# Cross-attention with image prompts on one core: the second batch's context turned on VectorE, prompts projected in four column tiles, its inner products ahead of the first products, and the last keys in two column tiles

## The chip, the cores and the metric

The kernel runs on one core of one Trainium2 chip. The metric is device time in microseconds (us) from the first to the last instruction of one execution, taken as the median of several executions. Three executions of the kernel before gave 419.8, 421.6 and 420.98 us: a median of 420.98 us.

## The reference: what is computed

Eight batches of 112 queries with 320 channels attend to 371 text rows and 4 prompt rows of a 512-channel context, in 20 heads of 16 channels. Beside the usual attention there is a second, small one over the 4 prompts. Its scores get an extra term: the cosine between the probability-weighted mean of the text rows (`qsem`) and each prompt.

```python
q, k_t, v_t = heads(x @ W_q), heads(text @ W_k), heads(text @ W_v)
probs_t  = softmax(q @ k_t.T * scale)            # 112 x 371 per head
text_out = probs_t @ v_t
qsem     = l2norm(probs_t @ text)                # 112 x 512 per head
fused    = q @ k_ip.T * scale + 0.5 * qsem @ l2norm(ip).T
probs_ip = softmax(fused) * spatial_mask         # 112 x 4 per head
out = (text_out + probs_ip @ v_ip) @ W_out + b_out + x
```

All data are float32. Every matmul of the program appears in the trace as two MATMUL records, each with its own weight load (a transpose through TensorE as one).

## The kernel before, in words

**Tiling.** `qsem` is never formed. Its length is p G p^T, with p a row of probabilities and G the 371 x 371 matrix of inner products of the context rows ("gram"). So each head needs one product of its turned probabilities with a tile `u` that holds, side by side, G, the products with the normalised prompts, a column of ones and the values. The 20 heads go in five groups of four (steps (b, g), g = 0 to 4). The four heads of a group sit in the four 32-row strips of the array and run beside each other.

**One step (b, g).** `scores` (L662) makes four score tiles from `kT` and the masked queries `qm`. `probabilities` takes the maximum on VectorE (L675) and the exponential on ScalarE (L679), and sends p to a tile `xg` by DMA on the SP queue (L686). `transposed` turns it on VectorE (`xgT`, L698). `product` (L710) is the large product in twelve blocks of 32 context rows. `reduced` multiplies the result by p and sums it on VectorE (L763); `value_sums` copies the small columns on ScalarE (L737). `placed` puts the values of the next step into `u` on GpSimd (L629). Scores run two steps ahead of products.

**Preparing a batch.** `load_ctx` loads the context. For batches 0 and 1 (`b < LEAD`) rows lie on partitions and `transposed_context` turns them by 12 transposes through TensorE with copies from PSUM on ScalarE and VectorE (L414, L422, L424). From batch 2 on it is loaded in 32 x 128 pieces and turned by three VectorE instructions (L402); then `prompts_behind` copies the four normalised prompt columns into the same tile on GpSimd (L390). `gram` (L474) makes G in three pieces, four column tiles of 32 wide beside each other, doubled on ScalarE (L460) and multiplied by `half` on GpSimd (L461), and `gram_to_groups` spreads it over strips of `u` by DMA (L488). `values` (L543) projects V in three chunks; `values_to_dram` and `values_to_groups` reorder it through DRAM. `keys` (L512) projects K in three blocks of 128 channels.

**The last 64 channels.** 320 channels are two full blocks and 64 channels more (heads 16 to 19). The kernel before spreads those four heads over four 32-row strips with zeros between (`spread`, L124). For batches 0 and 7 the third key block is a full 128-wide projection of spread weights (L512, and `last_keys`, L526). For batches 1 to 6 the 64 channels ride along with the values, which are 384 wide for that (L543), go to a spread tile `k3` on GpSimd (L552) and are turned by three TensorE transposes (L503).

**The prompts.** `prompt_projections` projects all 32 prompt rows with two weights, each into its own 32-wide column tile of one bank, 320 columns each (L280); the result goes to `kip` and to DRAM.

**What sets the order.** The order on every engine around the change is written out by hand (`manual_schedule`): an engine takes its instructions in program order and waits at each for the semaphores that it needs. The prologue does batch 0 and step (0, 0); `alone(0)` does the products of step (0, 0); `behind(n)` then does work for the next batch between the products of one step and of the next ones; `pair(n)` does the products of two steps. `turn` names the PSUM pools of the banks that come next. The SP queue has eight completion semaphores in rotation, so that a DMA is issued only when the one eight places ahead of it has landed.

**Lines of the prologue** that the prediction follows. SP loads context 0, the value weights, x of batch 0, the query and key weights and context 1 (L161 to L170). TensorE: gram of batch 0 (L444), values (L543), queries (L344) and keys (L512) of batch 0, scores (0, 0), context 1 (L414), scores (0, 1), two more key blocks, the first piece of gram 1; then the products of (0, 0), two more pieces of gram 1, the prompt projections (L280), a chunk of values 1 and the products of (0, 1). GpSimd clears 64 rows of `xT` (L327), which the third matmul of the first query block needs, and prepares weights.

## Time and profile before

| | |
|---|---|
| executions | 419.8, 421.6, 420.98 us; median 420.98 us |
| the profiled execution's own time | 421.54 us |
| its span, first to last instruction | 419.8 us (1.7 us lie around it) |
| mean granted TensorE clock | 0.999 |
| DMA | 64.64 MB in 58002 packets, 154 GB/s over the span |
| chain that ended last, by engine | PE 87%, DVE 4%, DMA 3%, ACT 2%, SPq 2% |

How to read it: PE is TensorE's matmuls, PEld its weight loads, DVE VectorE, ACT ScalarE, POOL GpSimd, SP SyncE, which issues DMAs here; SPq, ACTq and POOLq are the sequencers' own records, DMA issues above all. A row of the timeline gives start and length in us, engine, line, operation, output<-input, shape and count, and in brackets the idle time of that engine before it and what ended it. A row of the groups gives count, busy us, mean ns of one, idle time. Matmul records overlap, since they are pipelined, so the pace of a group is its busy time over its count, or the difference between the starts of two rows, and not the mean length of one record.

### The profile page before, as it was taken

To read this page: it belongs to the slowest core of one execution; us is meant where nothing else is said; L and a number is where in the kernel's file an instruction comes from. 1 tells how busy PE (TensorE), PEld (TensorE's weight loads), DVE (VectorE), ACT (ScalarE), POOL (GpSimd) and SP (SyncE) were. 2 spreads that over 40 slices of the span, in tenths; PEclk is the share of its full clock that TensorE was granted. 3 is DMA by queue.
4 is the path that set the end of the run, shared out by engine and by line. 5 is a ranking of instruction groups with operands and counts; after the bars stand their busy time and mean duration, and the time that the engine had idled before them with its cause. 6 is when DMAs were issued, how large, how long until landed. Compare 5 with 4: busy or idle time off the path is not lost.

```text
span 419.8 us, 13826 instructions
## 1 busy us (share of the span) xinstructions
PE 411.7 (98%) x5511; PEld 314.1 (75%) x5511; DVE 322.2 (77%) x684; ACT 185.5 (44%) x634; POOL 116.0 (28%) x278
## 2 busy tenths in 40 slices
PE   8999999999999999999999999999999999999995
PEld 8866686877677786868686877778776888776893
DVE  4054777897887876886888897887788897789964
ACT  3253333334543642514553464333643464246772
POOL 4302310031161352012051225102124126005570
PEclk9999999999999999999999999999999999999999
DMA  8678966778554656577645575575656345575311
GB/s 249 163 190 246 220 157 165 180 187 181 133 156 125 169 127 170 143 162 160 174 116 138 148 173 144 156 186 138 164 150 168 92 118 149 156 177 169 98 34 29
DMA packets 58002, 64.64 MB, mean 154 GB/s; under 512 B 19016, under 2 KB 51760, under 8 KB 57938
## 3 DMA queue, kind: packets, MB, share of 16 engines
q1 hardware_dynamic: 57054, 62.32, 58.5%
q8 instruction: 44, 0.72, 0.7%
q10 hardware_dynamic: 692, 0.89, 0.7%
q0 software_dynamic: 192, 0.55, 0.6%
q14 instruction: 20, 0.16, 0.1%
HBM read 19.04 MB, written 5.22 MB: 58 GB/s over the span
## 4 chain that ended last, share of the span: by engine, by line
PE 87%; DVE 4%; DMA 3%; ACT 2%; SPq 2%; issue 1%; ACTq 0%; POOL 0%; DVEq 0%; POOLq 0%
PE ps_qd L710 39%; PE ps_v L543 15%; PE ps_k L512 10%; PE ps_g L474 8%; PE ps_s L662 5%; PE ps_q L344 3%; PE ps_o L867 2%; DMA xg<-p 1%; DVE xgT L698 1%; PE ps_g L444 1%; DMA vr<-vd 1%; ACT p L679 1%; PE ps_c L414 1%; DVE nmx L675 1%; SPq L488 1%; DMA ct<-in_ctx_dram 1%
## 5 line engine op out<-in xcount | busy, mean ns | idle before, releaser
L710 PE MATMUL ps_qd<-u,xgT 32*112 32x40 f32 (+11 forms) x3840 | 215.7, 351 | 0.4 <-DVE xgT L698 0.4
L710 PEld LDWEIGHTS ps_qd<-u,xgT 32*112 32x112 f32 x3840 | 177.4, 172 | 38.4 <-issue 7.1
L698 DVE STREAM_TRANSPOSE xgT<-xg 128x768 f32<-128x768 f32 (+1 forms) x63 | 123.1, 1976 | 7.1 <-DMA xg<-p 7.1
L679 ACT ACTIVATE p<-ps_s,nmx 112x371 f32<-112x371 f32 x160 | 85.6, 584 | 58.3 <-DVE nmx L675 57.2
L675 DVE TENSOR_REDUCE nmx<-ps_s 112x1 f32<-112x371 f32 x160 | 77.1, 534 | 36.7 <-PE ps_s L662 34.0
L763 DVE CUSTOM_DVE_ANT_0 p<-ps_qd,p 112x371 f32<-112x371 f32 x150 | 72.7, 544 | 15.9 <-ACT pvs L737 10.4
L629 POOL COPY u<-vr 128x64 f32<-128x64 f32 x120 | 26.7, 236 | 185.0 <-PE ps_qd L710 108.0
L543 PE MATMUL ps_v<-wv_sb,ctxT 128*128 128x384 f32 (+1 forms) x192 | 63.8, 479 | 0.3 <-ACT kT L519 0.3
L662 PE MATMUL ps_s<-kT,qm 32*112 32x375 f32 (+1 forms) x320 | 60.8, 486 | 0.0
L543 PEld LDWEIGHTS ps_v<-wv_sb,ctxT 128*128 128x128 f32 x192 | 35.3, 190 | 21.2 <-ACT kT L519 1.2
L512 PE MATMUL ps_k<-ctxT,wk_sb 128*128 128x371 f32 x136 | 45.8, 481 | 0.0
L737 ACT COPY pvs<-ps_qd 112x21 f32<-112x21 f32 x150 | 21.7, 198 | 52.4 <-DVE ss L763 50.1
L512 PEld LDWEIGHTS ps_k<-ctxT,wk_sb 128*128 128x128 f32 x136 | 24.6, 190 | 13.4 <-ACT ctxT L424 0.5
L474 PE MATMUL ps_g<-ctxT 128*32 128x119 f32 (+11 forms) x672 | 33.3, 344 | 0.6 <-POOL ctxT L390 0.6
L474 PEld LDWEIGHTS ps_g<-ctxT 128*32 128x32 f32 x672 | 25.9, 109 | 8.1 <-issue 4.1
L662 PEld LDWEIGHTS ps_s<-kT,qm 32*112 32x112 f32 x320 | 27.1, 171 | 5.0 <-issue 0.5
L550 ACT COPY vext<-ps_v 128x384 f32<-128x384 f32 (+1 forms) x24 | 11.2, 465 | 37.1 <-PE ps_v L543 37.0
L681 ACT COPY ipl<-ps_s 112x4 f32<-112x4 f32 x140 | 24.0, 172 | 0.0
L353 DVE TENSOR_SCALAR qm<-ps_q,emask 128x224 f32<-128x224 f32 (+1 forms) x25 | 9.0, 398 | 18.5 <-PE ps_q L344 18.5
L460 ACT ACTIVATE ug<-ps_g 128x375 f32<-128x375 f32 (+2 forms) x24 | 9.0, 377 | 29.2 <-DMA ct<-in_ctx_dram 8.4
L519 ACT COPY kT<-ps_k 128x371 f32<-128x371 f32 x17 | 8.0, 469 | 30.5 <-PE ps_k L512 30.5
L402 DVE STREAM_TRANSPOSE ctxT<-ct 128x512 f32<-128x512 f32 x18 | 19.3, 1077 | 0.0
(157 smaller groups left out, 311.6 us busy)
## 6 DMA issues: line engine op xcount, KB each, us to landing
xg<-p SPq DMA_DIRECT2D x158, 162.3 KB
u<-ug SPq DMA_DIRECT2D x128, 99.0 KB
ct<-in_ctx_dram SPq DMA_DIRECT2D x24, 176.0 KB
vip<-vipd SPq DMA_DIRECT2D x7, 560.0 KB
vr<-vd SPq DMA_DIRECT2D x20, 120.0 KB
vd<-vext SPq DMA_DIRECT2D x14, 160.0 KB
vd<-vext SPq DMA_DIRECT2D x28, 40.0 KB
ct<-in_ctx_dram SPq DMA_DIRECT2D x4, 256.0 KB
```

The source lines that it names most:

```text
L474: nc.tensor.matmul(ps[p * RG : (p + 1) * RG, s0 : T - t0], ctxT[:, e, t0 + q * RG : t0 + (q + 1) * RG], ctxT[:, e, t0 + s0 : T], start=(e ...
L512: nc.tensor.matmul(ps[:, :TT], wk_sb[:, e, i * P : (i + 1) * P], s["ctxT"][:, e, :TT], start=(e == 0), stop=(e == NE - 1),)
L543: nc.tensor.matmul(ps[:, :w], ctxT[:, e, c * P : (c + 1) * P], wv_sb[:, e, :w], start=(e == 0), stop=(e == NE - 1),)
L629: nc.gpsimd.tensor_copy(region(b, c)[:, :, UV - c * P :], s["vr"][:, c * QN : (c + 1) * QN, g, :])
L662: nc.tensor.matmul(ps[:S, :w], qm[a * RG : (a + 1) * RG, i, r, j * S : (j + 1) * S], s["kT"][a * RG : (a + 1) * RG, i, :w], start=True, st ...
L675: nc.vector.tensor_reduce(nmx, ps[:S, :TT], AX.X, ALU.max, negate=True)
L679: nc.scalar.activation(p, ps[:S, :TT], AF.Exp, bias=nmx)
L681: nc.scalar.copy(s["ipl"][:, groups[g][a], :], ps[:S, TT:T])
L698: nc.vector.transpose(xT[:, j : j + n].rearrange("p j (k q) -> p q j k", q=QN), xg[:, :, j * RG : (j + n) * RG].rearrange("p q (j k) -> p ...
L710: nc.tensor.matmul(banks[a][:S, j * RG : UW], xT[a * RG : (a + 1) * RG, j, :S], region(b, c)[a * RG : (a + 1) * RG, p, q * RG :], start=(j ...
L737: nc.scalar.copy(s["pvs"][:, h, :], ps[:S, TT:UW])
L763: nc.vector.tensor_tensor_reduce(out=p, in0=ps[:S, :TT], in1=p, scale=1.0, scalar=0.0, op0=ALU.mult, op1=ALU.add, accum_out=s["ss"][:, h : ...
```

## The change

1. **Context 1** is loaded in pieces (eight DMAs on SP, runs of 512 bytes) and turned by three VectorE instructions, which stand right behind the first gram and ahead of everything else that VectorE does for batch 0. The 12 TensorE transposes and their three copies go. The copy of the prompts (`prompts_behind`) now stands on GpSimd ahead of the clearing of `xT`.
2. **Last keys.** For every batch the third key block is made by `last_keys`: the 64 channels against the two halves of the context rows, in two column tiles of 64 (8 matmuls of 186 or 185 columns), then four copies on ScalarE, each half to two places. The spread weights, `k3`, its transposes and the 64 further columns of the values go; `qm` gets a second mask for that block (one VectorE instruction more for each pair of batches).
3. **Prompt projections** in four column tiles of 160 columns (16 matmuls instead of 8 of 320), with three ScalarE copies and two DMAs to DRAM instead of one each.
4. **Gram of batch 1**: all three pieces ahead of the products of step (0, 0), instead of one ahead and two behind.
5. **Loads**: the prompt weights and x of batches 1 to 4 are issued by GpSimd during the first gram, instead of by SP after the first scores; x of batches 5 to 7 by GpSimd two batches later than before. The weight tiles are now 320 wide, so that a row of the key weights lands in one run.
6. **Sqrt table**: loaded by an instruction of its own right behind the last keys, ahead of where it was loaded.

```diff
     groups = [[i * HC + 2 * a + r for a in range(GROUP)] for i in range(2) for r in range(2)]
-    groups.append([2 * HC + a for a in range(GROUP)])
+    groups.append([2 * HC + 2 * (a % 2) + a // 2 for a in range(GROUP)])
...
-    wk_sb = const.tile([P, NE, CP], F32, tag="wk_sb", name="wk_sb")
-    wv_sb = const.tile([P, NE, C + REST], F32, tag="wv_sb", name="wv_sb")
+    wk_sb = const.tile([P, NE, C], F32, tag="wk_sb", name="wk_sb")
+    wv_sb = const.tile([P, NE, C], F32, tag="wv_sb", name="wv_sb")
...
     def load_ctx(b):
         ct = io.tile([P, NT, E], F32, tag="ct", name=f"ct_{b}")
-        if b >= LEAD:
+        if b > 0:
...
     def prompt_projections():
         ps = bank("ps_kv")
         for e in range(NE):
             for i, w in enumerate((wkip_sb, wvip_sb)):
-                nc.tensor.matmul(
-                    ps[i * N : (i + 1) * N, :C], ipT[:, e, :], w[:, e, :],
-                    start=(e == 0), stop=(e == NE - 1),
-                )
-        kv = work.tile([2 * N, C], F32, tag="vip", name="kv", bufs=1)
-        nc.scalar.copy(kv, ps[: 2 * N, :C])
+                for n, part in enumerate(parts):
+                    m = 2 * i + n
+                    nc.tensor.matmul(
+                        ps[m * N : (m + 1) * N, : C // 2], ipT[:, e, :], w[:, e, part],
+                        start=(e == 0), stop=(e == NE - 1),
+                    )
+        kv = work.tile([P, CP], F32, tag="vip", name="kv", bufs=1)
+        nc.scalar.copy(kv[:N, parts[0]], ps[:N, : C // 2])
+        nc.scalar.copy(kv[:N, parts[1]], ps[N : 2 * N, : C // 2])
+        nc.scalar.copy(kv[2 * N :, : C // 2], ps[2 * N :, : C // 2])
...
-            for r in range(2 if i < FULL else 1):
+            for r in range(2):
                 nc.vector.tensor_scalar_mul(
                     qm[:, i, r, : n * S], ps[:, : n * S], emask[:, r : r + 1]
                 )
...
     def first_gram():
...
             if c == NT - 1:
                 nc.gpsimd.tensor_copy(ctxT[:, :, TT:T], ipnT[:, :, :NIP])
+                load_embed(nc.gpsimd, wkip_sb, w_k_ip)
+                load_embed(nc.gpsimd, wvip_sb, w_v_ip)
+                nc.gpsimd.dma_start(x_sb[:, 1:5, :], x[1:5].rearrange("b s c -> s b c"))
...
     def last_keys(b, ps):
         s = st[b]
         for e in range(NE):
-            nc.tensor.matmul(
-                ps[:, :TT], wk_sb[:, e, FULL * P :], s["ctxT"][:, e, :TT],
-                start=(e == 0), stop=(e == NE - 1),
-            )
-        nc.scalar.copy(s["kT"][:, FULL, :TT], ps[:, :TT])
+            for n in range(2):
+                nc.tensor.matmul(
+                    ps[n * REST : (n + 1) * REST, : min((n + 1) * KH, TT) - n * KH],
+                    wk_sb[:, e, FULL * P :],
+                    s["ctxT"][:, e, n * KH : min((n + 1) * KH, TT)],
+                    start=(e == 0), stop=(e == NE - 1),
+                )
+        for n in range(2):
+            t = slice(n * KH, min((n + 1) * KH, TT))
+            for m in range(2):
+                nc.scalar.copy(
+                    s["kT"][m * REST : (m + 1) * REST, FULL, t],
+                    ps[n * REST : (n + 1) * REST, : t.stop - t.start],
+                )
...
     order_values()
     drain(products)
+    drain(transposed_context(1))
     gram_to_groups(0, range(QN - 1))
...
-    spread(nc.gpsimd, wq_sb)
-    nc.gpsimd.tensor_copy(wv_sb[:, :, C:], wk_sb[:, :, FULL * P : C])
-    spread(nc.gpsimd, wk_sb)
+    nc.gpsimd.tensor_copy(wq_sb[:, :, C:], wq_sb[:, :, FULL * P : C])
...
-    turn[:] = ["mm", "qd", "qd"]
-    drain(transposed_context(1))
-    prompts_behind(1)
     for a in range(GROUP):
         scores(0, 1, a, early=True)
         probabilities(0, 1, a)
-    load_embed(nc.sync, wkip_sb, w_k_ip)
-    load_embed(nc.sync, wvip_sb, w_v_ip)
...
     more_constants()
-    run(("g", 1), lambda: gram(1))
+    turn[:] = ["mm", "mm", "sc"]
+    run(("g", 1), lambda: gram(1), NT)
...
             if n == 0:
-                turn[:] = ["sc", "mm", "qd", "mm"]
-                nc.sync.dma_start(x_sb[:, 1:5, :], x[1:5].rearrange("b s c -> s b c"))
+                turn[:] = ["qd", "mm"]
             else:
                 turn[:] = ["qd"] * 4 + ["mm"]
                 k(b)
+                nc.scalar.preload_act_table(AF.Sqrt)
                 f(b - 1)
...
             tr(0)
-            gr(nb, 2)
             if n:
+                gr(nb, 2)
                 f(b - 1)
```

Here KH is 186, REST is 64 and `parts` are the two halves of the 320 channels. `keys`, which the diff leaves out here, now makes two full blocks and then calls `last_keys` for the third, for every batch but the last one, which calls it at the place where it did before.

More of the change, by code (lines that the diff above doesn't have):

```diff
@@ L241, in order_values @@
             )
-        nc.vector.tensor_copy(
-            wv_by[:, :, :, 2 * FULL, :],
-            wv_in[:, :, FULL * P :].rearrange("p e (a d) -> p e a d", d=D),
-        )
+        last = wv_in[:, :, FULL * P :].rearrange("p e (u v d) -> p e u v d", v=2, d=D)
+        for v in range(2):
+            nc.vector.tensor_copy(wv_by[:, :, 2 * v : 2 * v + 2, 2 * FULL, :], last[:, :, :, v, :])
+    parts = [slice(n * C // 2, (n + 1) * C // 2) for n in range(2)]
     def normalised_prompts():
@@ L310, in prompt_projections @@
         yield
-        nc.sync.dma_start(vipd, kv[N:])
+        for n, part in enumerate(parts):
+            m = 2 + n
+            nc.sync.dma_start(vipd[:, part], kv[m * N : (m + 1) * N, : C // 2])
         yield
@@ L956, in ending @@
             )
-        parts = [slice(i * C // 2, (i + 1) * C // 2) for i in range(2)]
         ps_o = [bank(f"ps_o_{b}_0", spare=True)]
```

81 lines of the change are left out of this document (26 added, 55 removed).

## The prediction

> **What bounds the kernel now.** I read the page first, then who waited for whom on TensorE, then its timeline over the first 50 us.
>
> ```profile
> PE 411.7 (98%) x5511; PEld 314.1 (75%) x5511; DVE 322.2 (77%) x684; ACT 185.5 (44%) x634; POOL 116.0 (28%) x278
> ```
> ```profile
> PE ps_g L474 <- POOL ctxT L390: 0.6, 1, 0.6
> PE ps_qd L710 <- DVE xgT L698: 0.4, 1, 0.4
> ```
>
> TensorE is busy for 411.7 of 419.8 us, and behind its start its longest wait is 0.6 us. So a matmul taken away is worth its length, unless the work behind it then waits for something that it covered. Where that is so is read from the start:
>
> ```profile
> 20.30 0.82 PE L344 MATMUL ps_q<-xT,wq_sb 128*128 128x112 f32 x6
> ...
> 25.91 1.59 PE L414 MATMUL ps_c<-ident,ct 128*128 128x128 f32 x12
> 27.43 1.28 PE L662 MATMUL ps_s<-kT,qm 32*112 32x371 f32 x8
> 28.64 5.25 PE L512 MATMUL ps_k<-ctxT,wk_sb 128*128 128x371 f32 x16
> 33.82 2.71 PE L474 MATMUL ps_g<-ctxT 128*32 128x375 f32 x32
> 36.46 1.22 PE L710 MATMUL ps_qd<-u,xgT 32*112 32x392 f32 x10
> ...
> 41.81 2.31 PE L474 MATMUL ps_g<-ctxT 128*32 128x247 f32 x64
> 43.91 2.36 PE L280 MATMUL ps_kv<-wip,ipT 128*32 128x320 f32 x16
> 46.21 2.85 PE L543 MATMUL ps_v<-wv_sb,ctxT 128*128 128x384 f32 x8
> 48.98 1.22 PE L710 MATMUL ps_qd<-u,xgT 32*112 32x392 f32 x10
> ```
> ```profile
> 25.82 1.95 ACT L679 ACTIVATE p<-ps_s,nmx 112x371 f32<-112x371 f32 x4 [0.52 <-DVE nmx L675]
> ```
> ```profile
> 32.74 3.12 DVE L698 STREAM_TRANSPOSE xgT<-xg 128x768 f32<-128x768 f32 x2 [2.51 <-DMA xg<-p]
> ...
> 42.11 0.54 DVE L763 CUSTOM_DVE_ANT_0 p<-ps_qd,p 112x371 f32<-112x371 f32 x1 [2.11 <-ACT pvs L737]
> ...
> 43.97 4.50 DVE L698 STREAM_TRANSPOSE xgT<-xg 128x1536 f32<-128x1536 f32 x2
> ```
>
> The products of step (0, 0) start at 36.46; their turned probabilities were ready at 32.74 + 3.12 = 35.86. Those of step (0, 1) start at 48.98, behind 7.2 us of other matmuls. VectorE needs nearly as long there: the reductions start at 42.11, the turn at 43.97.
>
> **The price of a column tile of 64.** No row shows one.
>
> ```profile
> L543 PE MATMUL ps_v<-wv_sb,ctxT 128*128 128x384 f32 x144 | 49.8, 492 | 0.0
> ...
> L543 PE MATMUL ps_v<-wv_sb,ctxT 128*128 128x320 f32 x48 | 14.0, 438 | 0.3 <-ACT kT L519 0.3
> ...
> L344 PE MATMUL ps_q<-xT,wq_sb 128*128 128x224 f32 x54 | 12.3, 364 | 0.0
> ...
> L964 PE MATMUL ps_o<-wo_sb,aT 128*112 128x160 f32 x12 | 2.0, 307 | 0.0
> ```
>
> Busy time over count is the pace: 0.346 us at 384 columns, 0.292 at 320, 0.228 at 224, 0.167 at 160, so about 0.19 at 186. The 16 records of L280, two 32-wide tiles of 320 columns in turn, started over 43.91 to 46.21: 0.144 each, half of 0.292. So two column tiles run beside each other. A call of the new `last_keys`, 16 records of 186 columns, is 16 x 0.19 / 2 = 1.5 us; 3.1 if its tiles stood in line, the upper end. The nearest row is two tiles with 128 rows, as here, so I take 1.5.
>
> ```profile
> 101.35 0.48 PE L503 MATMUL ps_k<-ident,k 128*128 128x128 f32 x3
> 101.67 2.67 PE L512 MATMUL ps_k<-ctxT,wk_sb 128*128 128x371 f32 x8
> ...
> 138.02 0.54 PE L503 MATMUL ps_k<-ident,k 128*128 128x128 f32 x3
> 138.49 4.71 PE L474 MATMUL ps_g<-ctxT 128*32 128x375 f32 x96
> ```
>
> The three transposes that go take 0.32 us between full-width neighbours (101.35 to 101.67) and 0.47 between two other tilings (138.02 to 138.49): a change of tiling costs some 0.15.
>
> [...]
>
> **Batches 1 to 7.** The values lose 64 columns in 18 chunks, 17 of them behind the start: 17 x 8 records x 0.054 = 7.3 us less. Six calls of `last_keys` come for the transposes: 6 x 1.5 - 3 x 0.32 - 3 x 0.47 = 6.6 more, and 3 x 0.15 for tilings between full-width blocks: 7.1. Together -0.2. In batch 7 a full third block becomes a call:
>
> ```profile
> 383.54 2.76 PE L526 MATMUL ps_k<-ctxT,wk_sb 128*128 128x371 f32 x8
> ```
> ```profile
> 378.35 0.49 DVE L873 TENSOR_TENSOR ob<-ps_o,xb 112x320 f32<-112x320 f32 x1 [0.29 <-PE ps_o L867]
> ...
> 389.41 1.64 DVE L698 STREAM_TRANSPOSE xgT<-xg 128x768 f32<-128x768 f32 x1
> ```
>
> That is 1.2 us less, but VectorE has no gap from 378.35 until this turn ends at 391.05, and the products of (7, 2) need it. These come behind those of (7, 1), which follow the key block at 386.2 and take the 5.3 us that 36.46 to 41.81 shows: at about 391.5. I count 0.3.
>
> **The start, if no load is late.** Twelve transposes go (25.91 to 27.43: 1.5). Two of the score tiles behind them lie in banks that the first two exponentials (25.82 and on, 0.49 each) free by 26.8, so I count 1.1. The third key block goes from 2.6 to 1.5, and 2.1 us of gram (41.81 to 43.91) come ahead. TensorE reaches the first products at 36.46 - 1.1 - 1.1 + 2.1 = 36.4, about as before. Behind these products stand only the prompts, in four tiles 2.3 x (0.167 / 0.292) = 1.3, less or more by 0.2, and one chunk of values, 2.3: TensorE is done at 41.8 + 3.6 = 45.4. VectorE keeps its order there: first reduction 42.1, turn 43.97.
>
> ```profile
> L698 DVE STREAM_TRANSPOSE xgT<-xg 128x1536 f32<-128x1536 f32 x17 | 51.5, 3027 | 0.0
> ```
>
> The turn ends at 47.0, so the next products start at 47.1: 1.9 us earlier than 48.98, of some 4 us of matmul time that has gone up to there. The moved gram was the cover of this turn; TensorE now waits 1.7 us there, a new wait on VectorE.
>
> **Small parts.** Four ScalarE copies of half the width for one, and one more `qm` instruction a pair, lie beside TensorE:
>
> ```profile
> L519 ACT COPY kT<-ps_k 128x371 f32<-128x371 f32 x17 | 8.0, 469 | 30.5 <-PE ps_k L512 30.5
> ...
> L353 DVE TENSOR_SCALAR qm<-ps_q,emask 128x224 f32<-128x224 f32 x15 | 6.1, 444 | 4.0 <-PE ps_q L344 4.0
> ```
>
> Four copies cost at most 4 x 0.47 - 0.47 = 1.4 us on an engine busy for 44%, and the keys of the last group are used two steps later: 0. The `qm` one may lengthen the 0.6 us wait for `ctxT`: +0.3. The table load keeps its count; it moves into ScalarE time beside gram: 0. SP is relieved of issues; what then stands first on it waits for probabilities: 0. Together: -0.2 - 0.3 - 1.9 + 0.3 = **-2.1 us**.
>
> **The load that VectorE now waits for.** The turn of context 1 stands on VectorE ahead of `qm` of batch 0, and on GpSimd the copy behind it stands ahead of the clearing of `xT`, without which the first query block (20.30) cannot end; keys and scores queue behind that.
>
> ```profile
> 8.47 0.20 POOL L440 COPY ctxT<-ipnT 128x16 f32<-128x16 f32 x1 [2.64 <-DVE ipnT L270]
> ...
> 14.56 0.28 POOL L327 MEMSET xT<- 64x224 f32 x1
> ...
> 47.13 0.92 POOL L118 DMA_DIRECT2D wo_sb<-in_L_xattn_W_out_dram  x1
> ```
> ```profile
> L402 DVE STREAM_TRANSPOSE ctxT<-ct 128x512 f32<-128x512 f32 x18 | 19.3, 1077 | 0.0
> ```
>
> Three turns (3.2), copy (0.2), clearing (0.3) and handing over (0.1) are 3.8 us; the third query matmul is due at about 20.6. So the context must land by **16.8**.
>
> ```profile
> 11.00:12.00 1.00, 1.00 (x12) 1.00 (x11) 0.00 (x0) 0.06 (x1) 0.00 (x0) 1.00 1.06 385
> ...
> 13.50:14.00 0.50, 0.50 (x4) 0.42 (x4) 0.00 (x0) 0.27 (x1) 0.24 (x1) 1.00 0.02 8
> ```
> ```profile
> q1 hardware_dynamic: 833, 0.41, 119.8%
> ```
> ```profile
> q0 software_dynamic: 36, 0.18, 81.2%
> q1 hardware_dynamic: 85, 0.04, 26.1%
> ```
>
> Before, all first loads are in at 13.5 (8 GB/s from there). Now context 1 is 1484 packets of 512 bytes. Of the same kind SP's queue moved 833 in the 2 us from 48 to 50, 417 a us: 3.6 us behind the key weights, from about 10.5 to 14.1. But GpSimd issues 1.85 MB behind its copy at 8.47. Its issue at 47.13 had moved hardly a packet by 50, so these start at about 11.5, with 1070 packets of the context left. In the us from 50.5 both queues ran: 36 packets of GpSimd's took 81% of the engines' time, and SP's fell to 85. At that rate (0.18 MB a us) the prompts need until 21.8, and the context lands at 22.3; at the 385 GB/s (0.385 MB a us) of the us from 11 they need 4.8 us, until 16.3; by then the context has moved another 410 packets, the other 660 take 1.6, and it lands at 17.9. I take 18.3, near the latter, since the prompts' weights come in long runs (5120 bytes): a wait of 1.5 us. Its bounds are 0 (landing at 14.1) and 5.5.
>
> **Sum:** -2.1 + 1.5 = -0.6 us against the profiled execution's own 421.54 (span 419.8 and 1.7 around it). The median of the runs is 420.98, 0.56 below it; against the median: **420.4 us**.
>
> **Rivals.**
> - *No wait:* the context lands by 16.8, as it would by equal shares of bytes: 0.55 MB of each queue in 1.1 MB at 0.23 MB a us, 4.8 us, at 16.3. Then -2.1, 418.9. Against it stands 0.18 to 0.04 MB in the last rows. [...] Chance 0.27.
> - *Slower:* the context shares the engines as in the us from 50.5 and lands at 22.3: a wait of 5.5, +3.4, 424.4. From 18.9 on the kernel is slower than before. For it: the only rows of both queues. Against: they are shorter runs, at the end of a load. Chance 0.14.
> - *The tiles of 64 stand in line*, the change doesn't do what it says: 8 x 1.6 = 12.8 more, some hidden: about 431. L280 speaks against it. Chance 0.03.
> - *The wait on the turn at 47 us doesn't come*, or the calls are cheaper (1.3): 417.6. Chance 0.08.
>
> **How the numbers follow.** The forecast, a landing between 17 and 20, keeps 0.48: 419 to 422. The range, **417.9 to 423.6**, takes in no wait and most of the slow landing; beyond lie some 0.06 below and 0.12 above. Bounds at 0.5%, about what a measurement here can tell from no change, are 418.9 and 423.1. Faster: half of *no wait*, the last rival, a little of the forecast: 0.28. Slower: most of *slower*, and *in line*: 0.13. Within: 0.59.
>
> **What would show it.** In the timeline after: a TensorE gap before the third matmul of L344's first block at 20 to 23 us, ended by GpSimd's clearing (none if *no wait*); a wait of 1 to 2 us of the products of (0, 1) on `xgT`; 64-row key records at a pace of 0.09; gram in one piece of 4.7 us ahead of the first products; the products of (7, 2) waiting on VectorE. The forecast is wrong if the landing is outside 17 to 20, or if key records come at 0.19.

## The result and the profile after

The changed kernel takes 424.71 us (median of five executions, 423.26 to 426.46); the kernel before, run beside it, 420.58 us (five, 419.61 to 421.60). The ratio is 1.0106, with a 95% interval of 1.0080 to 1.0132: **slower by about 1%**, outside the range of 417.9 to 423.6. The profiled execution took 424.67 us, with a span of 422.9 us against 419.8. All ratios here and below are taken over fast executions; one of e3's seven (429.7 us) was a slow one.

From the page of the changed kernel, the busy line and the granted clock over 40 slices of 10.6 us:

```profile
PE 411.1 (97%) x5609; PEld 319.7 (76%) x5609; DVE 327.1 (77%) x692; ACT 190.4 (45%) x658; POOL 114.7 (27%) x267
...
PEclk9969999999999999999999999999999999999999
```

TensorE is busy for as long as before, but in the third slice its clock is at 0.6. The timeline of that stretch (start and length in us; the bracket is the idle time before it and what ended it):

```profile
20.32 2.07 DVE L393 STREAM_TRANSPOSE ctxT<-ct 128x512 f32<-128x512 f32 x2 [9.78 <-DMA ct<-in_ctx_dram]
...
23.51 1.08 DVE L393 STREAM_TRANSPOSE ctxT<-ct 128x512 f32<-128x512 f32 x1 [1.12 <-DMA ct<-in_ctx_dram]
24.66 0.20 POOL L381 COPY ctxT<-ipnT 128x16 f32<-128x16 f32 x1 [9.53 <-DVE ctxT L393]
24.92 0.28 POOL L319 MEMSET xT<- 64x224 f32 x1
...
25.25 0.77 PE L336 MATMUL ps_q<-xT,wq_sb 128*128 128x112 f32 x2 [3.74 <-POOL xT L319]
...
30.79 1.12 PE L336 MATMUL ps_q<-xT,wq_sb 128*128 128x112 f32 x6
```

This is the wait that the prediction placed there, by the chain that it named: the pieces of context 1 land at 20.3, their tails of 19 rows only at 23.5, the last turn ends at 24.6, and GpSimd's copy and clearing follow. In the windows of 1 us the granted clock is the third column from the end, ahead of the DMA share and GB/s:

```profile
24.00:25.00 1.00, 0.00 (x0) 0.00 (x0) 0.60 (x1) 0.00 (x0) 0.28 (x2) 0.79 1.09 368
25.00:26.00 1.00, 0.75 (x3) 0.75 (x4) 0.00 (x0) 0.00 (x0) 0.55 (x2) 0.50 0.87 230
...
30.00:31.00 1.00, 1.00 (x4) 0.54 (x2) 0.00 (x0) 0.00 (x0) 0.00 (x0) 0.50 1.05 231
31.00:32.00 1.00, 1.00 (x10) 0.89 (x13) 0.05 (x1) 0.47 (x1) 0.00 (x0) 0.80 0.12 25
```

The clock falls to half within the wait and stays there until 31.4, some 6 us after work has come back. The first key block, 2.6 us before, takes from 25.82 to 30.79: 5.0. From there on:

```profile
37.91 1.48 PE L511 MATMUL ps_k<-ctxT,wk_sb 128*64 128x186 f32 x16
39.32 4.71 PE L468 MATMUL ps_g<-ctxT 128*32 128x375 f32 x96
...
43.95 1.22 PE L696 MATMUL ps_qd<-u,xgT 32*112 32x392 f32 x10
...
50.21 1.29 PE L273 MATMUL ps_kv<-wip,ipT 128*32 128x160 f32 x32 [0.83 <-DVE ss L749]
...
54.57 1.22 PE L696 MATMUL ps_qd<-u,xgT 32*112 32x392 f32 x10 [0.71 <-DVE xgT L684]
...
407.99 5.04 PE L696 MATMUL ps_qd<-u,xgT 32*112 32x392 f32 x96 [0.83 <-DVE xgT L684]
```

The first products start at 43.95 instead of 36.46, **+7.5 us**; those of (0, 1) at 54.57 instead of 48.98, +5.6; the last ones at 407.99 instead of 403.27, +4.7. So the whole loss lies ahead of 44 us, and 2.8 us are won back after it. The spans differ by 3.1 only: behind the last output's issue the profiled execution of the kernel before took 1.6 us longer to end than this one, and no other profiled execution, of either kernel, has that. The medians, 4.1 apart, are nearer to the 4.7.

### The profile page after: what moved, and what is told of

It reads as the page before. It is cut to its first block, busy times and chain, and to the rows that moved or that the text cites. A ratio compares the mean times of both kernels' runs of the same rounds, so it can differ in the third digit from the quotient of the medians.

```text
span 422.9 us, 14048 instructions
## 1 busy us (share of the span) xinstructions
PE 411.1 (97%) x5609; PEld 319.7 (76%) x5609; DVE 327.1 (77%) x692; ACT 190.4 (45%) x658; POOL 114.7 (27%) x267
## 4 chain that ended last, share of the span: by engine, by line
PE 83%; DVE 7%; DMA 6%; issue 1%; ACT 1%; ACTq 0%; SPq 0%; POOL 0%; DVEq 0%; POOLq 0%
PE ps_qd L696 40%; PE ps_v L533 11%; PE ps_k L494 10%; PE ps_g L468 8%; PE ps_s L648 6%; PE ps_q L336 3%; DVE xgT L684 3%; DMA ct<-in_ctx_dram 2%; PE ps_k L511 2%; PE ps_o L853 2%; DMA wk_sb<-in_L_xattn_W_k_dram 2%; DVE p L749 1%; DMA xg<-p 1%; DMA ip_sb<-in_ctx_dram 1%; DVE nmx L661 1%
## 5 line engine op out<-in xcount | busy, mean ns | idle before, releaser
L533 PE MATMUL ps_v<-wv_sb,ctxT 128*128 128x320 f32 x192 | 56.1, 439 | 0.3 <-ACT kT L501 0.3
L393 DVE STREAM_TRANSPOSE ctxT<-ct 128x512 f32<-128x512 f32 x21 | 22.3, 1070 | 10.9 <-DMA ct<-in_ctx_dram 10.9
L540 ACT COPY vext<-ps_v 128x320 f32<-128x320 f32 x24 | 10.2, 427 | 35.8 <-PE ps_v L533 33.3
L336 PE MATMUL ps_q<-xT,wq_sb 128*128 128x224 f32 (+1 forms) x90 | 18.1, 339 | 3.7 <-POOL xT L319 3.7
L336 PEld LDWEIGHTS ps_q<-xT,wq_sb 128*128 128x128 f32 x90 | 15.1, 199 | 6.1 <-POOL xT L319 3.9
L454 ACT ACTIVATE ug<-ps_g 128x375 f32<-128x375 f32 (+2 forms) x24 | 9.1, 379 | 23.2 <-PE ps_g L468 11.2
```

What stands on the lines that cost most here:

```text
L336: nc.tensor.matmul(ps[:, : n * S], wq_sb[:, j, i * P : (i + 1) * P], xT[:, j, : n * S], start=(j == 0), stop=(j == NC - 1),)
L533: nc.tensor.matmul(ps[:, :C], ctxT[:, e, c * P : (c + 1) * P], wv_sb[:, e, :], start=(e == 0), stop=(e == NE - 1),)
```

## The experiments

Seventeen runs. In each ratio "before" is the kernel before, run on the same chip beside the run; the groups of runs had different chips, so ratios compare better than times.

**My theory after the result:** GpSimd's loads make context 1 late (the wait that the prediction placed there, with a later landing), and the wait then halves the clock, a price of its own. **Rivals:** the context is late by its own short packets; the clock fell for another reason; the loads take something else as well.

### e1: the loads back on SP

```diff
-                load_embed(nc.gpsimd, wkip_sb, w_k_ip)      # in first_gram
-                load_embed(nc.gpsimd, wvip_sb, w_v_ip)
-                nc.gpsimd.dma_start(x_sb[:, 1:5, :], ...)
+    load_embed(nc.sync, wkip_sb, w_k_ip)                    # behind scores (0, 1)
+    load_embed(nc.sync, wvip_sb, w_v_ip)
...
+                nc.sync.dma_start(x_sb[:, 1:5, :], ...)     # behind step (0, 0)
```

> The changed kernel with GpSimd's three loads (prompt weights, x of batches 1 to 4) put back on SP where the kernel before had them, behind the scores of (0, 1) and behind (0, 0). Theory (contention): these 1.88 MB share the DMA engines with the second context and make it late; without them its last part lands by 16, TensorE doesn't wait before the first query block (3.7 us after the change), its granted clock stays at 1.00 up to 30 us, the first products start about 7 us earlier than 43.95, and the time is about 417.5. Rival (the load itself): the context's own packets of 512 bytes and the pace of SP's issues make it late; then it lands after 19 here too, the wait is over 2 us, and the time stays at 423 to 425.

422.64 us (ten executions, 420.65 to 424.12); ratio to before 1.0033 (1.0011 to 1.0056). The start went as expected: timeline of VectorE, then of TensorE:

```profile
16.29 3.09 DVE L393 STREAM_TRANSPOSE ctxT<-ct 128x512 f32<-128x512 f32 x3 [6.53 <-DMA u<-ug]
```
```profile
36.05 1.22 PE L693 MATMUL ps_qd<-u,xgT 32*112 32x392 f32 x10
...
47.12 1.22 PE L693 MATMUL ps_qd<-u,xgT 32*112 32x392 f32 x10
```

The context is in by 16.3, there is no wait, and the first products come 7.9 us earlier than after the change. **The loads made it late.** These two starts are the prediction's 36.4 and 47.1. But the time fell by 2 us (3 by the ratios, 1.0106 to 1.0033), and not by 7. At 86 us TensorE is 2.7 us ahead of the kernel before; then:

```profile
90.80 1.56 DVE L681 STREAM_TRANSPOSE xgT<-xg 128x768 f32<-128x768 f32 x1 [5.17 <-DMA xg<-p]
```
```profile
93.80 7.03 PE L693 MATMUL ps_qd<-u,xgT 32*112 32x392 f32 x55 [2.01 <-ACT ipl L664]
```
```profile
94.00:95.00 1.00, 1.00 (x11) 0.76 (x12) 1.00 (x2) 1.00 (x5) 0.00 (x0) 0.57 0.63 177
...
100.00:101.00 1.00, 1.00 (x15) 1.00 (x12) 0.00 (x0) 0.00 (x0) 0.24 (x1) 0.52 0.84 191
```

VectorE waits 5.2 us for probabilities, TensorE 2.0 for what follows on that, and again the clock is at half, for 7 us: from 2.7 us ahead at step (1, 0) it is 3.8 behind at (1, 2). Not every execution has that fall: in the two of ten whose mean clock was 0.999 or more, e1 took 421.14 and 420.69. Neither theory had this second loss; e5 to e17 look for its cause.

### e2: the clearing ahead of the turn

```diff
-    drain(transposed_context(1))
...
     nc.gpsimd.tensor_copy(wq_sb[:, :, C:], wq_sb[:, :, FULL * P : C])
+    drain(transposed_context(1))
```

> The changed kernel with the turns of the second context and GpSimd's copy behind them issued after the clearing of xT and the copy of wq, and still ahead of qm on VectorE; every load is as after the change. The context stays late (20 to 24 us). Theory (queue position): the lost time comes from the clearing behind the late context; now only qm is behind it, and TensorE waits about 1.2 us for a bank at the second query block instead of 3.7. If the clock fell because of the long wait, it stays up, and the time is about 418.5. Rival (the loads take something else as well, such as the late keys or u): the wait goes and the time stays above 421.

422.69 us (ten); 1.0035 (1.0010 to 1.0059). The first query block and key block now run on time, and the wait is at the second query block, not 1.2 us but 4.35:

```profile
27.62 1.62 PE L336 MATMUL ps_q<-xT,wq_sb 128*128 128x112 f32 x6 [4.35 <-ACT qT L349]
```

The turns still stand on VectorE ahead of `qm`; here they ended at 26.8, and the bank that TensorE needs next is freed behind `qm`. I had counted on a last turn at 24.6. Moving one thing out of the chain left the other in it, and the time is far from the 418.5 that I expected. (The profiled execution took 424.74, 2 us above the median.)

### e3: a filler in the wait

```diff
+    awake(17)          # 17 matmuls of 128 x 128 by 128, results not used
     run(("q", 0), None)
```

> The changed kernel with 17 matmuls of 128x128 by 128 columns, whose results aren't used (3.7 us at 0.22 each), on TensorE ahead of the first query block. The context is as late and the block ends no earlier, but TensorE isn't idle while it waits. Theory (the clock is a price of its own): the granted clock, 0.5 to 0.77 from 24 to 33 us after the change, stays near 1.00, the first key block takes 2.6 us instead of 5.0, and the time falls by 3 to 4, to about 421. Rival (the clock fell for another reason, or the slow key block is due to the loads): the block still takes 4 to 5 us and the time is 424 to 426.

423.02 us (seven); 1.0045 (1.0019 to 1.0071), 1.7 less than after the change (2.6 by the ratios; I had expected 3 to 4). In this execution the context landed still later, and 1.9 us of wait were left behind the filler:

```profile
26.52 0.47 PE L336 MATMUL ps_q<-xT,wq_sb 128*128 128x112 f32 x2 [1.88 <-POOL xT L319]
26.83 2.67 PE L494 MATMUL ps_k<-ctxT,wk_sb 128*128 128x371 f32 x8
...
42.20 1.22 PE L696 MATMUL ps_qd<-u,xgT 32*112 32x392 f32 x10
```

The key block takes 2.5 us (to 29.34), at a clock of 1.00 throughout. From the end of the wait to the first products it is 15.7 us here and 18.7 after the change: **the fall of the clock costs 3.0 us by itself**, and it comes from the wait.

### e4: the tails first

```diff
-            mains()                 # the four pieces (L136)
-            tails()                 # the four tails (L141)
+            for part in (tails, mains) if b == 1 else (mains, tails):
+                part()
```

> The changed kernel with the second context's four tails of 19 rows issued on SP ahead of its four pieces of 352 rows, the rest of the load unchanged. After the change the pieces landed at 20.3 and the tails only at 23.5. Theory (shared bandwidth, order of issue): all is in by about 20.5 to 21.5, the last turn ends near 24, and the wait of 3.7 us becomes 2.5 to 3.2; the clock still falls, and the time is about 423. Rival (the tails are late for a reason of their own, such as the wait of the issuing queue for a free place): nothing changes, 424.7.

426.87 us (four); 1.0150 (1.0117 to 1.0182). Both expectations missed: TensorE's wait grew to 5.3 us. VectorE:

```profile
23.23 3.00 DVE L400 STREAM_TRANSPOSE ctxT<-ct 128x512 f32<-128x512 f32 x3 [12.38 <-DMA u<-ug]
```

All of the context lands at 23.2 in this order as the last of it did at 23.5; only, with the large pieces last, no turn can be done earlier. So the tails aren't late for a reason of their own: what stands last in SP's queue while GpSimd's loads move is late. By 15.0 us, 191 of the context's 1484 packets of 512 bytes had started here, and 1384 after the change.

### e5, e6, e7: the loads later, gram split, turn first

```diff
     nc.gpsimd.tensor_copy(wq_sb[:, :, C:], wq_sb[:, :, FULL * P : C])
+    load_embed(nc.gpsimd, wkip_sb, w_k_ip)        # e5, e6, e7: here, not in first_gram
+    load_embed(nc.gpsimd, wvip_sb, w_v_ip)
+    nc.gpsimd.dma_start(x_sb[:, 1:5, :], ...)
...
-    run(("g", 1), lambda: gram(1), NT)            # e6: two pieces behind step (0, 0)
+    run(("g", 1), lambda: gram(1))
...
+            transposed(*steps[1], 0, BLK)         # e7: ahead of reduced(0, 0)
```

The order on VectorE in e7, and in e10, e13 and e16 below, goes with another bank for the projections (`turn`).

> The changed kernel with GpSimd's three loads still on GpSimd, but issued behind the copy of the second context, the clearing of xT and the copy of wq, so about 20 us instead of 9 to 11. The run with the loads put back on SP had no wait at the start, first products at 36.05 and those of (0, 1) at 47.12, but lost it again at 92 to 101 us: VectorE waited 5.2 us for probabilities, TensorE then 2.0, and its clock fell to 0.50 for 7 us. Theory (SP's queue): that second loss came from the load of x and the prompt weights standing on SP again, ahead of the third context and of probabilities; with the loads off SP and behind the second context neither loss is there: TensorE has no wait over 1 us behind its start, its clock stays at 1.00, and the time is about 417. Rival (the probabilities' way through SP and DRAM is simply no faster, and TensorE being 2.7 us ahead must wait for it): the wait of 2 us and the fall of the clock near 92 us come again, and the time is 421 to 423.

> As the run with the later loads, but with the inner products of batch 1 as before the change: one piece ahead of the first products, two behind them. Theory (my prediction's step: moved, they no longer cover VectorE's turn for (0, 1), so the move gives nothing by itself): the first products start 1 to 2 us earlier than there, those of (0, 1) within 0.7 us of it, and the time is within 0.6 us. Rival (work ahead of the first products is worth its length, since TensorE is busy): without the move (0, 1) starts 1.5 to 2 us later, and the time is up by as much.

> As the run with the later loads, but VectorE turns the probabilities of (0, 1) ahead of the four reductions of (0, 0) instead of behind them, and the prompts' projections take a bank that doesn't wait for a reduction. Theory (VectorE's chain of reductions and turn bounds the products of (0, 1)): they start about 1 us earlier than there, and the time falls by about 1. Rival (the probabilities themselves come late from DRAM, or TensorE's own work bounds there): no change, or up to 1 us slower.

425.67 us (five), 1.0100 (1.0067 to 1.0133); 425.05 (six), 1.0090 (1.0056 to 1.0123); 424.27 (nine), 1.0058 (1.0032 to 1.0084). Theory of e5 missed: no wait at 20 us and none at 92, but this one, of e5:

```profile
41.59 2.25 PE L693 MATMUL ps_qd<-u,xgT 32*112 32x392 f32 x10 [5.18 <-POOL u L611]
...
54.79 1.22 PE L693 MATMUL ps_qd<-u,xgT 32*112 32x392 f32 x10 [0.71 <-DVE xgT L681]
```

Loads that start at 20.7 run into the values and the probabilities of the first step, and the products wait for these. In e6 the wait was 6.9 and the products of (0, 1) started at 55.00, 0.2 from e5's: the moved inner products gave nothing, though the longer wait makes this weak. In e7 (0, 1) came 11.5 us behind (0, 0) instead of 13.2, so VectorE's chain does bound that place; the time fell by 1.4, as expected.

### e8 to e11: other places for the loads

```diff
     loaded[1] = load_ctx(1)
+    load_embed(nc.sync, wkip_sb, w_k_ip)          # e8, e9, e10
+    load_embed(nc.sync, wvip_sb, w_v_ip)
+    nc.sync.dma_start(x_sb[:, 1:5, :], ...)       # e9
...
     more_constants()
+    nc.gpsimd.dma_start(x_sb[:, 1:5, :], ...)     # e8, e10; e11 on top of e1
```

> The changed kernel with the prompt weights (1.31 MB) loaded on SP directly behind the second context, in the same queue, ahead of the copies of u, and x of batches 1 to 4 (0.57 MB) on GpSimd at about 36 us. Loads at 9 us made the context late, loads at 20 us made vr and the probabilities late (a wait of 5.2 us at 41), loads on SP at 36 and 43 us made the third context and later probabilities late (a wait of 2.0 us at 92): theory, the DMA engines are the start's second bound, and what counts is which transfer is made late. From 14 to 22 us they are busy for only 0.5 to 0.75 of the time, so behind the context in the same queue the weights delay only u, which is needed at 34. Then the context lands by 16.5, TensorE has no wait over 1 us behind its start, and the time is about 417. Rival (there is no free place: the start moves a fixed amount of data before the products, and any order makes one of them late): a wait of over 2 us comes somewhere before 100 us, and the time is 421 or more.

> As the run with the prompt weights behind the second context, with x of batches 1 to 4 behind them on SP too, so 1.88 MB instead of 1.31 in that place. Theory: x isn't needed before 57 us; there it adds 2 us to the delay of u, vd and vr. If these have that much to spare the time is the same as there within 0.5; if not, the first products wait for vr (GpSimd's copy into u), as they did with the loads at 20 us, and the time is 1 to 5 us more.

> As the run with the prompt weights behind the second context, and VectorE turns the probabilities of (0, 1) ahead of the reductions of (0, 0), with the projections in a bank that waits for no reduction. Theory (VectorE's chain bounds the products of (0, 1), by about 1 us): they start 0.7 to 1.5 us earlier than there, and the time falls by about as much, unless a later wait takes it back. Rival (the way of the probabilities through SP bounds the first 100 us, not VectorE): no gain by the end.

> The run with the loads put back on SP, but for x of batches 1 to 4, which GpSimd loads at about 36 us. It tells what made the second loss there (a wait of 2.0 us and a clock of 0.50 from 94 to 101). Theory (x stood on SP ahead of the third context and the probabilities): the wait and the fall of the clock go, and the time is 417 to 418. Rival (the prompt weights at 36 us and the data at large keep the DMA engines full from 38 to 56 us): the probabilities of (0, 3) are late as before, the wait at 92 comes again, and the time stays at 421 to 423.

| | us | ratio to before | the wait that came (from the profile) |
|---|---|---|---|
| e8 | 421.24 (ten) | 1.0012 (0.9989 to 1.0035) | 2.8 at 39.5, for the last copies of `u` |
| e9 | 426.41 (four) | 1.0121 (1.0099 to 1.0142) | 6.6 at 43.2, the same |
| e10 | 421.45 (ten) | 1.0011 (0.9993 to 1.0030) | 3.0 at 40.1, the same |
| e11 | 423.69 (six) | 1.0038 (1.0001 to 1.0075) | 3.6 and 3.4 at 46 and 50, for the prompt weights |

The rows behind the first and the last line of the table, of e8 and of e11:

```profile
39.46 1.24 PE L695 MATMUL ps_qd<-u,xgT 32*112 32x392 f32 x10 [2.79 <-POOL u L613]
```
```profile
46.06 0.75 PE L273 MATMUL ps_kv<-wip,ipT 128*32 128x160 f32 x4 [3.59 <-DMA wip<-in_L_xattn_W_k_ip_dram]
```

e8 and e10 are the best places for these loads so far, 3.3 to 3.5 us less than after the change, but every place took its wait somewhere: the rival held. e9 is 5.2 us slower than e8, where 1 to 5 were expected. e10's gain at (0, 1), 1.1 us, was gone by the end. In e11 x, issued on GpSimd's queue at 37.1, was in 8.7 us later, ahead of the prompt weights on SP's, issued at 37.6 and 38.2 and in at 46.1 and 50.2.

### e12, e13: half of u's copies off SP

```diff
-    gram_to_groups(0, range(QN - 1))
+    gram_to_groups(0, range(2))
...
+    gram_to_groups(0, range(2, QN), nc.gpsimd)    # on top of e8 (e13: of e10)
+    drain(transposed_context(1))
```

> As the run with the prompt weights behind the second context, but the copies of u for blocks 2 and 3 (8 of 16, 99 KB each) are issued by GpSimd at about 16 to 22 us, behind its clearing of xT and copy of wq, and ahead of its copy for the second context. SP then has 8 copies less ahead of vr and of the probabilities of (0, 0); in the run before, the probabilities were issued at 29.8, the last copies of u at 33.5 to 37.2, and TensorE waited 2.8 us for them, with its clock at 0.5 to 0.65 afterwards. Theory (order in SP's queue): probabilities issued by 28, first products at 36.0 to 36.5, no wait over 1 us and no fall of the clock, products of (0, 1) near 47.2, and about 416.5 to 417.5 us, below the kernel before. Rival (the data as such): the DMA engines are full in turn, another transfer is late, a wait of over 2 us comes before 100 us, and the time is 420 to 423.

> As the run with half of u's copies on GpSimd, and VectorE turns the probabilities of (0, 1) ahead of the reductions of (0, 0), with the prompts' projections in a bank that waits for no reduction. Theory (VectorE's chain bounds (0, 1)): its products start up to 1 us earlier than in that run; the end is earlier by as much if nothing later waits, so 415.5 to 417.5. Rival (the way of the probabilities bounds the rest of the start): (0, 1) starts earlier, and a later wait takes it back.

422.46 us (twelve), 1.0023 (1.0000 to 1.0045), and 421.79 (twelve), 1.0009 (0.9983 to 1.0035). The theory fell: a wait of 2.5 us (e12; 3.2 in e13) stood at the first products again. Of e12, SP, then TensorE:

```profile
29.89 1.89 SPq L566 DMA_DIRECT2D vr<-vd  x4
31.88 14.39 SPq L671 DMA_DIRECT2D xg<-p  x12
```
```profile
39.78 1.22 PE L695 MATMUL ps_qd<-u,xgT 32*112 32x392 f32 x10 [2.54 <-POOL ug L454]
```

Now the values came late through DRAM, and the probabilities stood behind them on SP: out at 31.9 instead of the 28 that I expected. The clock didn't fall in this execution (420.89 us); in most of the twelve it did.

### e14 to e17: what made the second loss of e1

SP's queue in e1 (start, length, issues), from 51.81 on:

```profile
51.81 5.32 SPq L669 DMA_DIRECT2D xg<-p  x4
57.56 3.58 SPq L479 DMA_DIRECT2D u<-ug  x4
61.23 3.63 SPq L669 DMA_DIRECT2D xg<-p  x4
64.91 5.03 SPq L479 DMA_DIRECT2D u<-ug  x8
69.99 2.14 SPq L304 DMA_DIRECT2D vipd<-kv  x2
72.17 2.75 SPq L555 DMA_DIRECT2D vd<-vext  x6
75.03 3.76 SPq L669 DMA_DIRECT2D xg<-p  x4
78.83 2.48 SPq L479 DMA_DIRECT2D u<-ug  x4
81.36 2.15 SPq L564 DMA_DIRECT2D vr<-vd  x4
83.61 3.66 SPq L669 DMA_DIRECT2D xg<-p  x4
```

44 issues fill 34.5 of the 35.5 us up to 87.3 (1.75 of the first row are a wait for the third context; from 57.56 on there is no gap). The probabilities at 83.61 are those that VectorE waits for at 90.8; they can't go out earlier, however far TensorE is ahead.

```diff
-                gram_to_groups(nb, (g - 1,))
+                gram_to_groups(nb, (g - 1,), nc.gpsimd if (b, g) == (0, 2) else nc.sync)
...
-            gram_to_groups(nb, (2,))
+            gram_to_groups(nb, (2,), nc.gpsimd if b == 0 else nc.sync)
...
-                turn[:] = ["qd", "mm"]                    # e17, behind (0, 0)
+                turn[:] = ["mm", "qd"]
+                v(nb)
...
+                v(nb)
             else:
                 run(("pp",), prompt_projections)
-            v(nb)
```

The first two edits are e14 (on top of e1), e15 (on the kernel before) and e16 (with e7's order on VectorE); the rest is e17, on top of e14.

> The run with the loads put back on SP, with 8 of the 16 copies of u for batch 1 (blocks 1 and 2, issued from 64.9 to 69.9 us there) on GpSimd's queue, which is idle there. Theory (SP's issues bound the stretch from 52 to 87 us): the probabilities that went out at 83.6 go out 3 to 5 us earlier, VectorE's wait of 5.2 us for them and TensorE's of 2.0 go, the clock stays at 1.00, the products that began at 93.80 begin near 91.6, and the time is 416 to 417.5, faster than both kernels. Rival (the data as such, or the way of the values through DRAM): the copies leave SP, the probabilities still land after 90, and the time stays at 421 to 423.

> The kernel before with the same 8 copies of u on GpSimd's queue. Theory (SP's issues bound only a kernel whose TensorE is ahead): nothing waits for these issues there, so the time stays within 0.5 us of before. Rival (SP or GpSimd's issues cost or save time by themselves): over 1 us faster or slower.

> The run with SP relieved, and VectorE turns the probabilities of (0, 1) ahead of the reductions of (0, 0), with the projections in a bank that waits for no reduction. Theory (VectorE's chain bounds (0, 1)): its products start up to 1 us earlier than in that run (47.1) and the end comes as much earlier. Rival (the prompt weights, which land at 43.5 there, hold TensorE at the projections in any case): no change.

> The run with SP relieved, with the first chunk of the values of batch 1 (2.3 us, ready) ahead of the prompts' projections on TensorE, in a bank that waits for no reduction. There TensorE waited 0.8 us for a bank and 2.4 for the prompt weights, and the products of (0, 1) began at 49.39. Theory (the wait for the weights stood in the path, and VectorE's turn at about 47 is the next bound): these waits fall to under 0.8 together, the products of (0, 1) begin at 47.1 to 47.6, and the time falls by about 2, to 416.5 to 417. Rival (a TensorE that is 2 us ahead waits for the probabilities behind SP again, near 92 us): the gain is lost there, and the time is 418 to 420.

| | us | ratio to before |
|---|---|---|
| e14 | 418.72 (nine) | 0.9932 (0.9899 to 0.9965) |
| e15 | 420.60 (ten) | 0.9971 (0.9945 to 0.9996) |
| e16 | 420.60 (ten) | 0.9967 (0.9939 to 0.9996) |
| e17 | 419.32 (twelve) | 0.9957 (0.9934 to 0.9979) |

**e14 beats both kernels**, by 0.7% the one before, though less than expected (416 to 417.5 us). Its probabilities went out at 82.43, 1.2 us earlier than in e1 where 3 to 5 were expected; VectorE waited 0.8 us for them, TensorE not at all, and its clock stayed at 1.00:

```profile
88.65 1.58 DVE L681 STREAM_TRANSPOSE xgT<-xg 128x768 f32<-128x768 f32 x1 [0.76 <-DMA xg<-p]
```

Where the 0.7% lie the traces don't show. In the profiled executions the products of (1, 2) start at 109.40 in e14 and at 109.43 before, the last ones at 403.12 and 403.27; e14's, at 419.63 us, is 0.9 above its median.

Nor is it a clean proof of what made e1's loss: TensorE had waited 2.4 us at 43.4 for the prompt weights, so it was no longer ahead. e17 takes that wait away, with the values in front:

```profile
47.33 1.22 PE L693 MATMUL ps_qd<-u,xgT 32*112 32x392 f32 x10 [1.59 <-DVE xgT L681]
```

Here TensorE is 1.7 us ahead at (0, 1), nearly as in e1, and there is no wait over 1.6 us behind it. From (0, 1) to (1, 2) it gave back 1.5 us, where e1 gave back 5.6. So SP's issues made most of that loss, the fall of the clock that came with it included. Of what is left, 1.3 us fall in the step at (0, 3), whose products take 12.0 us instead of 10.7 without a wait of TensorE's over 0.2. VectorE's turn there waited 2.1 us for a DMA. Whether that is the cause wasn't tried. The end was no earlier than e14's, as the rival of e17 said; the 416.5 to 417 of its theory were missed.

e15 was expected within 0.5 us; it is 0.3% (0.04 to 0.55%) faster. Its trace shows nothing of that: from the first products to those of (1, 2) it takes 72.97 us (35.96 to 108.93), just as before (36.46 to 109.43). So whether the relief alone gives part of e14's gain stays open. e16 is slower than e14, although it stood at the prompt weights for less time (1.9 us against 2.4): there the clock fell to half for 3.4 us, from 44.8, and in e14 it didn't (how the two waits lay is in the last section).

## Why the prediction was wrong, step by step

- **What bounds the kernel.** Right from 44 us on. For the start it was too simple: there a transfer ends each wait, and the sum treated the DMA side as one landing time.
- **The price of a call of the last keys**, 1.5 us: 1.41 measured (37.91 to 39.32). Two column tiles run beside each other: in line, by the prediction's estimate from the paces of other widths, the 16 records would have taken 3.1.
- **Batches 1 to 7**, -0.2, with batch 7's -0.3 and the small +0.3: between the products of (0, 1) and those of (7, 4) lie 354.29 us before and 353.42 after, -0.9. But that stretch scatters from one execution to the next: it takes 353.1 (e3) to 356.0 (e17) in the runs of the changed kernel without a fall of the clock in it, and 355.3 in e15, the order of before. So neither the sign nor the size is shown.
- **The start without a late load**: first products at 36.4, those of (0, 1) at 47.1. In e1, where the load isn't late, 36.05 and 47.12. From first products to (0, 1) -1.9 was forecast; after the change it is 10.62 instead of 12.52. Right, though of the wait of 1.7 us for VectorE only 0.7 stands at `xgT`; 0.8 stands at the projections, whose bank a reduction had to free, which the prediction hadn't seen.
- **The load that VectorE now waits for: the step that failed.** "I take 18.3 [...]: a wait of 1.5 us." The pieces landed at 20.3 and the tails at 23.5, past even the bound of 22.3. (That it cost 3.74 and not the 6.7 that a landing at 23.5 gives by the prediction's 3.8 us is because two of the three turns were done before the tails came.) GpSimd's loads, of which the prediction had the last in by 16.3 to 21.8, landed at 18.6, 21.2 and 24.0 (issue and time to landing: 9.22 + 9.4, 9.95 + 11.2, 10.49 + 13.5):

```profile
wip<-in_L_xattn_W_k_ip_dram POOLq DMA_DIRECT2D x1, 640.0 KB, 9.4
wip<-in_L_xattn_W_v_ip_dram POOLq DMA_DIRECT2D x1, 640.0 KB, 11.2
x_sb<-in_x_dram POOLq DMA_DIRECT2D x1, 560.0 KB, 13.5
```

  The wrong term is the rate of SP's queue beside GpSimd's. Both bounds let the context go on at 85 packets a us, with 1070 packets still to move when GpSimd's loads begin at 11.5. By the trace these began at 13.6, and by 15.0 all but 100 of the context's 1484 packets had started. But from 15 to 19 us GpSimd's queue (q0) had the engines almost alone, and SP's (q1) moved 53 packets in 4 us (packets, MB, share of the 16 engines):

```profile
q0 software_dynamic: 269, 1.24, 98.1%
q1 hardware_dynamic: 53, 0.03, 4.2%
```

  The last 100 packets took until 22.8; in e1, where q0 is empty, the last one starts at 16.1. So a few short packets at the end of the load made the wait, not its mean rate. The copies of `u`, which SP issues from 15.15 on, are not what held them up to there: their first packet moves at 19.5. Why the engines served the two queues like this no run shows.
- **What it left out: the clock.** The wait of 1.5 us was priced at its length. The measured one cost 3.74 and then 3.0 for the clock (e3). Of the 6.05 us by which the first products are later than forecast (43.95 against 36.4 + 1.5), 2.2 are the longer wait, 3.0 the clock (half of the 6.16 us of work from 25.25 to 31.41 would be 3.1), and 0.6 were there at 14.15 already, where the values began at 13.53 before; in the other runs they began between 13.03 and 14.27, so that is an execution's scatter.
- **"SP is relieved of issues [...]: 0."** Wrong as a rule. With the loads back on SP (e1) the issues of that queue decide what a TensorE that is 2.7 us ahead can keep. Whether the early loads of the change would have cleared the way there isn't shown: no run has them and a TensorE that is ahead.
- **The rivals.** *Slower* named the mechanism, and its 424.4 is 0.3 from the median; it got 0.14, because its rows, the only ones of both queues at work, were taken for a poor measure, as shorter runs (35 of GpSimd's 36 packets there are of 5120 bytes too). They were nearer than the calm average, and still too kind to SP's queue. That its time fits is partly luck: the loss came as 3.7 us of wait and 3.0 of clock, and not as 5.5 of wait. *No wait* missed by the step above; its equal shares of bytes are not what the trace shows, where from 15 to 19 us GpSimd's queue moved 1.24 MB and SP's 0.03. The last two did not come: a call measured 1.41, and the wait at (0, 1) is there, in two parts.

## What to carry to other kernels

When a load is moved earlier, sum all that the DMA engines have to move until the load in front of it must land, take the rows in which both queues are at work, and ask when the last packet gets through and not only the mean rate. Price a long wait of TensorE with the clock: here a wait that lasted 3.7 us cost 6.7. And where the first step is mended, look for the next queue that has no gap: in e1 TensorE was 2.7 us ahead, and lost it behind SP's issues and in the fall of the clock that came of them.

## What the runs showed of the hardware

- **Half the clock after a wait.** In each profiled execution the granted clock changes only on a grid of 3.413 us (after the change it is at half for 6.827 us and at full for the 392.533 behind them, 2 and 115 steps; before, at full for 413.013, 121 steps), whose start differs from one execution to the next (a step begins at 41.39 in e16, at 23.15 in e3), and behind a wait it stays at half for one step (3.4 us: e8, e10, e13, e16), two (6.8: after, e1, e4, e5, e7, e9) or three (10.2: e2, e6, e11). The falls went not with the length of a wait but with how much of it lay in one step. In all 13 falls ahead of the last matmul TensorE had been idle for 1.94 us (e16) or more of the step before; no step with 1.88 (e3) or less was followed by one. The wait of 1.94 in e16 was followed by half the clock, and the longer ones of 2.41 in e14 and 2.54 in e12, each split over two steps, were not. Steps of e16, e3 and e14 (second column PE busy; the clock is the third from the end):

```profile
41.39:44.81 3.42, 1.48 (x48) 1.11 (x44) 3.42 (x8) 0.41 (x4) 0.47 (x2) 1.00 0.98 273
44.81:48.22 3.41, 3.41 (x31) 2.21 (x32) 0.35 (x2) 0.85 (x3) 0.51 (x3) 0.50 1.08 209
```
```profile
23.15:26.56 3.41, 1.53 (x15) 1.35 (x13) 2.72 (x3) 0.00 (x0) 0.50 (x3) 1.00 0.80 231
26.56:29.97 3.41, 3.41 (x16) 2.44 (x16) 0.58 (x2) 0.68 (x2) 0.32 (x1) 1.00 0.73 172
```
```profile
44.18:47.59 3.41, 1.76 (x30) 1.39 (x31) 2.99 (x3) 0.42 (x2) 0.00 (x0) 1.00 0.99 215
47.59:51.01 3.42, 3.42 (x27) 2.04 (x30) 1.61 (x2) 0.85 (x3) 2.87 (x6) 1.00 1.21 194
```

  The clock came back only behind a step in which TensorE was never idle; in e1 and e2 it needed two of them, and why isn't shown. Nor was the step in front of a fall always idle as a whole: of the 3.41 us in front of e16's, TensorE was busy for 1.48.
- **An issue on SP** took, in e1 from 57.56 to 87.3, where the queue has no gap, between 0.46 us (`vd`, 2.75 for 6) and 0.94 (`xg`, 3.76 for 4); eight of `u` took 0.63 each (5.03).
- **GpSimd's queue against SP's.** After the change, from 15 to 19 us, GpSimd's packets of 5120 bytes took 98% of the engines' time and SP's 4%; in e4, from 13 to 15, 84% and 13%. In e11, x (560 KB) was issued on GpSimd at 37.1 us; the prompt weights, issued on SP at 37.6 and 38.2, were in at 46.1 and 50.2. In e1 they were issued at 36.2 and 36.8, with no x beside them, and the last was in at 43.6.
